# Taking the mean of the attention output out of the output weights, and the layer-norm statistics onto ScalarE

## Chip, cores and metric

The kernel runs on one core of one Trainium2 chip. The metric is device time in microseconds (us) of one execution; lower is better. TensorE is called PE, VectorE DVE, ScalarE ACT, GpSimd POOL and SyncE SP, as in the profile. SP issues nearly all the DMAs; ACT issues a few.

## What is computed

The input `x` has 2048 tokens of 1024 channels, in float32. One block of single-head attention with head size 256 is followed by a gated feed-forward layer (1024 to 2752 to 1024). Each has a layer norm (without gain or shift) before it and a second one on its output, ahead of the residual sum:

```python
def _layernorm(x, axis=-1, eps=1e-05):
    m = jnp.mean(x, axis=axis, keepdims=True)
    v = jnp.var(x, axis=axis, keepdims=True)
    return (x - m) / jnp.sqrt(v + eps)
...
    x = x + _layernorm(_L0_attn_ref(_layernorm(x, axis=-1), L0_attn_Wqkv, L0_attn_bqkv, L0_attn_Wo, L0_attn_bo), axis=-1)
    x = x + _layernorm(_L0_ffn_ref(_layernorm(x, axis=-1), L0_ffn_W_gate, L0_ffn_W_up, L0_ffn_W_down), axis=-1)
```

The attention ends with `out @ Wo + bo`, and the feed-forward layer computes `(silu(x @ W_gate.T) * (x @ W_up.T)) @ W_down.T`. In what follows, *a* is the attention output of a token (after `Wo` and `bo`), *x1* is `x + layernorm(a)`, and *xn* is `layernorm(x1)`, the input of the feed-forward layer.

## The kernel before

All large products run as three float32r matmuls on operands that are split into a high and a low part: `split` (L111, L112) copies the high part on ACT (a CAST) and subtracts it on DVE. So each weight or activation block that PE reads costs one ACT and one DVE instruction.

**Stages.** First come the projections to q, k and v with the statistics of `x` (row mean and scale of each token, kept in SBUF by `m_of` and `r_of`), up to about 140 us. Then comes attention over 16 tiles of 128 tokens (`i`, up to about 410 us). Then the feed-forward layer runs in two halves of 1024 tokens; in each, `gate_up` runs over ten pairs `p` of weight blocks (in the first half about 410 to 795 us), and `run_down` follows. Products of the feed-forward layer are arranged as in Strassen's scheme, which needs sums of blocks on DVE (L883, L791 to L794).

**One attention tile.** `scores`, `softmax` (exp on ACT, L443), `turn` (PE transposes, then split), `attend`, `turn_o` (L478, split at L480 and L481) and `proj` (the product with `wo_s`, the split `Wo`; DVE scales it and adds `bo_s`, L491) give *a*. `wo_split` makes `wo_s` from `wr`, pinned into the programs of tiles 0 and 1.

**From a to xn.** `out_stats` takes mean and scale of *a* by `norm_stats` (two bn_stats L118, bn_aggr L121, a small add L122 on DVE, a power L123 on POOL, then L499 on POOL). `residual` applies them on ACT (L505), adds `x` (L506), stores *x1* (L507), takes the statistics of *x1* in the same way, and writes *xn* on ACT (L510). `spread` (ACT's DMA, L597) and `gather` (SP's DMA, L600) pass *xn* through DRAM, `xpose` transposes it on DVE (L604, pinned) and stores it (L606).

The first eight tiles (`t < EARLY`, with EARLY = 8) do this inside the attention loop, two tiles behind. The last eight store *a* to DRAM (`at_d`) and are done later, one in each of the pairs p = 1 to 8 of the first half of the feed-forward layer. There `ahead(p)` transposes tile p-1 and loads *a* (L1308) and `x` (L1309) of tile p into two rooms that swap roles at each p, so that the load of *a* needs the room that `xpose` has just read, and the load of `x` the one that `xpose` wrote and L606 stores. `behind(p)` runs `residual` and `spread`, and `between(p)` the `gather`.

**One pair of gate_up.** Fourteen products of twelve matmuls each use four PSUM banks, `ag, au, cg, cu`. The part that matters here:

```python
        prod(ag, wg, "S3", "T3", False)
        nc.scalar.copy(g22, ag)
        add(g22, cg, g22)
        silu(g22, g22)
        prod(au, wu, "S3", "T3", False)
        nc.scalar.copy(u22, au)
        ...
        prod(ag, wg, "A22", "T4", False)
```

The copies L931 (`g22`) and L935 (`u22`) read a bank that PE needs again one product later.

**Order.** The order on each engine is fixed when the program is built, by a scheduler with its own timeline of the kernel, except where an instruction is pinned (`pin`, `tc.keep_in_program_order`). Weight loads and their splits are queued by `Feeder`, as buffers come free. The chip then runs each engine's instructions in that order.

Of the kernel before, what the change touches and what calls it, by code (L numbers as in the profile page):

```python
# [10 lines left out]
AF = mybir.ActivationFunctionType  # L11
ALU = mybir.AluOpType
# [5 lines left out]
C = 1024  # L18
# [6 lines left out]
TB = G // P  # L25
# [3 lines left out]
EPS = 1e-5  # L29
# [5 lines left out]
def block_kernel(ctx, tc, x, xt, wqk, wqk_t, wv, bqk, bv, wo, bo, wgu, wlast, wd, out):  # L35
# [12 lines left out]
    nc = tc.nc  # L48
# [4 lines left out]
    def tl(p, shape, dt, name):  # L53
        return p.tile(shape, dt, tag=name, name=name, bufs=1)
# [7 lines left out]
    bo_s = tl(cpool, [P, C], F32, "bo_s")  # L62

    mhalf = tl(cpool, [P, 16], F32, "mhalf")[:, 0:1]
# [7 lines left out]
    def small_tile():  # L72
        small_n[0] += 1
        return small[small_n[0] % NSM]

    bank_pool = pool("banks", space=PSUM)
    bank = [tl(bank_pool, [P, 512], F32, f"bank{i}") for i in range(8)]
# [29 lines left out]
    def f32(ap):  # L107
        return ap.bitcast(F32)

    def split(hi, lo, src, lo_engine=None):  # L110
        nc.scalar.copy(hi, src)  # L111
        (lo_engine or nc.vector).tensor_tensor(lo, src, f32(hi), ALU.subtract)  # L112

    def norm_stats(halves, pin=None):

        s = small_tile()
        for i, h in enumerate(halves):
            b = nc.vector.bn_stats(s[:, 6 * i : 6 * i + 6], h)  # L118
            if pin:
                pin(b)  # L120
        nc.vector.bn_aggr(s[:, 12:14], s[:, 0:12])  # L121
        nc.vector.tensor_scalar(s[:, 14:15], s[:, 13:14], EPS, None, ALU.add)  # L122
        nc.gpsimd.tensor_tensor(s[:, 15:16], s[:, 14:15], mhalf, ALU.pow)  # L123
        return s[:, 12:13], s[:, 15:16], s

    def mm3(o, w, m, first, last, pin=lambda i: i):

# [38 lines left out]
    pin = tc.keep_in_program_order  # L166
    L, R = slice(0, 512), slice(512, 1024)
# [19 lines left out]
    def m_of(g, tb):  # L187
        return yg[g][:, 2 * tb : 2 * tb + 1]
# [69 lines left out]
    def scores(i, j, pin=lambda i: i):  # L258

        cols = slice((i % TB) * P, (i % TB + 1) * P)  # L260
        q = qa if i < TB else qs[(i // TB) % 2]
        for d in range(2):
            k = kT(d, j)
            mm3(bank[j], (q[:, d, 0, cols], q[:, d, 1, cols]), (k[:, 0, :], k[:, 1, :]), d == 0, d == 1, pin)
        nc.vector.tensor_reduce(ys[i % 4][:, j : j + 1], bank[j], AX.X, ALU.max)
# [8 lines left out]
    def wv_pair(j):  # L274

        r = wv_raw[j // 2][:, (j % 2) * 512 : (j % 2) * 512 + 512].rearrange("p (c f) -> p c f", f=D)
        return wv_s[:, 2 * j : 2 * j + 2, 0, :], wv_s[:, 2 * j : 2 * j + 2, 1, :], r
# [54 lines left out]
    for c in range(2):  # L332
        h, l, r = (t[:, c, :] for t in wv_pair(0))
# [86 lines left out]
    wo_s = wvo.rearrange("p a b c -> p (a b c)").rearrange("p (d h c) -> p d h c", d=2, h=2)  # L420
    pT = [a2[:, 4 * i : 4 * i + 4, :, :].rearrange("p a b c -> p (a b c)").rearrange("p (k h q) -> p k h q", h=2, q=P) for i in range(2)]
    o_s = [f2[4][:, 0:D], f2[4][:, D:]]
    EARLY = 2 * TB
# [5 lines left out]
    def q_load(g):  # L429
        nc.sync.dma_start(qraw, q_d[g])  # L430

    def q_split(g, pin=lambda i: i):
        q = qs[g % 2]
        pin(nc.scalar.copy(q[:, :, 0, :], qraw))
        nc.vector.tensor_tensor(q[:, :, 1, :], qraw, f32(q[:, :, 0, :]), ALU.subtract)

    def softmax(i):

        s = ys[i % 4]
        nc.vector.tensor_reduce(s[:, 4:5], s[:, 0:4], AX.X, ALU.max)  # L440
        nc.vector.tensor_scalar(s[:, 5:6], s[:, 4:5], -1.0 / 16.0, None, ALU.mult)
        for j in range(4):
            nc.scalar.activation(p_s[:, j * 512 : j * 512 + 512], bank[j], AF.Exp, bias=s[:, 5:6], scale=1.0 / 16.0, accum_out=s[:, 8 + j : 9 + j])  # L443
        nc.vector.tensor_reduce(s[:, 12:13], s[:, 8:12], AX.X, ALU.add)
        nc.vector.reciprocal(s[:, 13:14], s[:, 12:13])

    def turn(i, j):

        b = bank[(4, 7)[j % 2]]
        for n in range(4):  # L450
            k = 4 * j + n
            nc.tensor.transpose(b[:, n * P : (n + 1) * P], p_s[:, k * P : (k + 1) * P], ident)  # L452
        d = pT[i % 2][:, 4 * j : 4 * j + 4, :, :]
        split(d[:, :, 0, :], d[:, :, 1, :], b.rearrange("p (n q) -> p n q", n=4))
# [29 lines left out]
    def proj(i):  # L484
# [8 lines left out]
            nc.sync.dma_start(at_d[i], a)  # L493
        return m

    def out_stats(t, a):

        m, r, s = norm_stats([a[:, 0:512], a[:, 512:1024]], tc.keep_in_program_order if t >= EARLY else None)
        nc.gpsimd.tensor_scalar(s[:, 16:17], m, r, -1.0, ALU.mult, ALU.mult)  # L499
        return r, s  # L500

    def residual(t, a, xt, st=None, pin=lambda i: i):

        r, s = st or out_stats(t, a)
        pin(nc.scalar.activation(a, a, AF.Identity, bias=s[:, 16:17], scale=r))  # L505
        (nc.gpsimd if t >= EARLY else nc.vector).tensor_tensor(xt, xt, a, ALU.add)  # L506
        nc.sync.dma_start(x1_d[t].rearrange("(g s) c -> s g c", g=4), xt)  # L507
        m, r, s = norm_stats([xt[:, 0:512], xt[:, 512:1024]])
        nc.gpsimd.tensor_scalar(s[:, 16:17], m, r, -1.0, ALU.mult, ALU.mult)
        nc.scalar.activation(a, xt, AF.Identity, bias=s[:, 16:17], scale=r)  # L510

    cols = lambda g, n: load_cols(g, 2 * n, 2, col_room[g][n])
    parts = lambda g: [x_parts(g, 2 * n, 2, col_room[g][n]) for n in range(4)]
# [59 lines left out]
    wr = [tl(wpool, [P, C], F32, f"wr{i}") for i in range(2)]  # L573
# [4 lines left out]
    xe = tl(spool, [P, C], F32, "xe")  # L578
# [8 lines left out]
    for d in range(2):  # L587
        nc.sync.dma_start(wr[d], wo[d * P : (d + 1) * P, :])

    def wo_split(d):  # L590
        pin(nc.scalar.copy(wo_s[:, d, 0, :], wr[d]))
        pin(nc.vector.tensor_tensor(wo_s[:, d, 1, :], wr[d], f32(wo_s[:, d, 0, :]), ALU.subtract))


    def spread(t, a):

        nc.scalar.dma_start(xn_d[t].rearrange("(i s) (g c) -> i s g c", i=4, g=4).rearrange("i s g c -> (s g) i c"), a.rearrange("p (i c) -> p i c", i=4))  # L597

    def gather(t, b):
        nc.sync.dma_start(b, xn_d[t])  # L600

    def xpose(t, a, b):

        pin(nc.vector.transpose(a.rearrange("p (j g s) -> p j g s", j=8, g=4), b.rearrange("p (g j c) -> p j g c", g=4, j=8)))  # L604
        d = xT_d[t // TB][:, (t % TB) * P : (t % TB + 1) * P]
        nc.sync.dma_start(d.rearrange("(j p) t -> p j t", p=P), a.rearrange("p (j t) -> p j t", j=8))  # L606
# [29 lines left out]
    L, R = slice(0, 512), slice(512, 1024)  # L636
# [22 lines left out]
    pin = tc.keep_in_program_order  # L659
# [77 lines left out]
    class Slot:  # L737
        t = None
# [466 lines left out]
    for i in range(NT):  # L1205
        more = i + 1 < NT
        if i % TB == 0 and TB <= i < NT - TB:
            q_load(i // TB + 1)
        if 3 <= i < EARLY + 3:
            gather(i - 3, pair[i % 3][1])  # L1210
        turn(i, 0)
        turn(i, 1)
        if i == NT - 1:
            for f in order[:2]:
                f.use()
            for f, r in zip(order[4:6], f4[2:4]):
                f.load(r)
        if more:
            scores(i + 1, 0)
            scores(i + 1, 1)  # L1220
        turn(i, 2)
        turn(i, 3)
        if more:
            scores(i + 1, 2)
            scores(i + 1, 3)
            softmax(i + 1)

        if i < 2:
            wo_split(i)
        if i == 1:  # L1230
            q_load(1)
        if i == 2:
            q_split(1, pin)
        if i % TB == 0 and TB <= i < NT - TB:
            q_split(i // TB + 1, pin)
        if 2 <= i < EARLY + 2:
            residual(i - 2, *pair[(i - 2) % 3], sts[i - 2], pin)
            spread(i - 2, pair[(i - 2) % 3][0])
        if i < 3:
            nc.sync.dma_start(pair[i][1], x[i * P : (i + 1) * P, :])  # L1240
        if i == NT - 1:
            for f in order[2:5]:
                f.use()
            for f, r in zip(order[6:8], (wr[1], f4[1])):
                f.load(r)
        if i > 0:
            turn_o(i - 1)
        attend(i)
        if i > 0:
            proj(i - 1)  # L1250
        if 3 <= i < EARLY + 3:
            xpose(i - 3, *pair[i % 3])
        if 3 <= i < EARLY:
            nc.sync.dma_start(pair[i % 3][1], x[i * P : (i + 1) * P, :])
        if 0 < i <= EARLY:
            sts[i - 1] = out_stats(i - 1, pair[(i - 1) % 3][0])
        cb = i - EARLY - 3
        if 0 <= cb < 4:
            first_sums(cb, *room[cb % 2])
        if 0 <= cb + 1 < 4:  # L1260
            first_load(cb + 1, *room[(cb + 1) % 2])
        if i == NT - 4:
            feed.pump()
        if i == NT - 2:
            for n in range(2):
                slots.free(flat(a2[:, 2 * n : 2 * n + 2, :, :]))
            feed.pump()
            order = [t2[0], t13[0], t13[1], t13[2], t2[1], t13[3]] + t4
            spare = f4[2], f4[3], wr[1], xe
            for f, r in zip(order, spare):  # L1270
                f.load(r)
# [129 lines left out]
```

## Time and profile before

| | |
|---|---|
| median of 3 runs | 1645.23 us (1644.34 to 1645.7) |
| the profiled execution | 1644.92 us, of which span 1643.1 us |
| PE busy | 1633.6 us (99%) |
| DVE busy | 1122.5 us (68%) |
| ACT busy | 718.2 us (44%) |
| POOL busy | 108.7 us (7%) |
| granted PE clock | 1.000 over the span |

The span runs from the first to the last instruction on the core; 1.82 us of the profiled execution's time lie around it. Busy time is the time in which an engine's own instructions ran. In a timeline each row has the start, the duration, the engine and line, and in brackets how long the engine had been idle before and what ended that idle time.

### The profile page before, as it was taken

How to read it: one execution, taken by the hardware profiler on the slowest of the kernel's cores; microseconds unless marked ns; L12 is line 12 of the kernel's file. 1: busy time of each engine (PE TensorE's matmuls, PEld its weight loads, DVE VectorE, ACT ScalarE, POOL GpSimd, SP SyncE). 2: the span in 40 equal slices, each digit the busy share in tenths (PEclk: the TensorE clock that was granted, in tenths of full speed). 3: DMA queues.
4: the chain of work that ended last, by engine and by line, in shares of the span. 5: the costliest groups of instructions: out<-in, count | busy, mean ns of one | idle time of the engine just before them, and what ended most of it. 6: DMA issues, size and time to landing. Idle time of an engine off the chain costs nothing.

```text
span 1643.1 us, 20860 instructions
## 1 busy us (share of the span) xinstructions
PE 1633.6 (99%) x7576; PEld 1361.1 (83%) x7576; DVE 1122.5 (68%) x1676; ACT 718.2 (44%) x1061; POOL 108.7 (7%) x157
## 2 busy tenths in 40 slices
PE   9999999999999999999999999999999999999998
PEld 8888888888888888888888888888888888888887
DVE  6656787778778888787577458855666655455458
ACT  5663445436444444433465344433333333354342
POOL 3120000000011111120000001100000000000001
PEclk9999999999999999999999999999999999999999
DMA  9452145556657777677477657532222333686663
GB/s 324 164 178 69 52 158 189 167 199 210 232 172 242 252 252 246 227 237 264 156 250 248 195 182 236 199 104 96 97 96 96 103 103 121 242 260 195 192 190 121
DMA packets 148184, 300.38 MB, mean 183 GB/s; under 512 B 14576, under 2 KB 39792, under 8 KB 148080
## 3 DMA queue, kind: packets, MB, share of 16 engines
q1 hardware_dynamic: 138480, 288.69, 53.1%
q10 hardware_dynamic: 9600, 10.36, 2.0%
q8 instruction: 59, 0.97, 0.2%
q14 instruction: 45, 0.37, 0.1%
HBM read 206.70 MB, written 92.29 MB: 182 GB/s over the span
## 4 chain that ended last, share of the span: by engine, by line
PE 94%; DVE 2%; DMA 2%; issue 1%; ACT 0%; POOL 0%; SPq 0%; POOLq 0%; DVEq 0%; ACTq 0%
PE bank L869 71%; PE bank L128 4%; PE bank L130 4%; PE bank L129 4%; PE bank L468 3%; PE bank L469 2%; PE bank L452 2%; PE bank L246 1%; PE bank L247 1%; PE bank L311 1%; DVE a L112 0%; DMA f<-xn_d 0%; DMA f<-wv 0%; DMA xn_d<-f 0%; PE bank L1056 0%
## 5 line engine op out<-in xcount | busy, mean ns | idle before, releaser
L869 PE MATMUL bank<-a 128*128 128x512 f32 (+1 forms) x960 | 226.4, 386 | 0.0
L869 PE MATMUL bank<-xb,a 128*128 128x512 f32 x912 | 212.5, 389 | 0.1
L869 PEld LDWEIGHTS bank<-a 128*128 128x128 f32 x960 | 179.1, 188 | 36.6
L869 PEld LDWEIGHTS bank<-xb,a 128*128 128x128 f32 x912 | 170.9, 188 | 35.8 <-DVE a L112 0.5
L111 ACT CAST a<-f2p 128x1024 fp32r<-128x1024 f32 (+2 forms) x123 | 106.9, 869 | 124.7 <-PE bank L869 89.5
L112 DVE TENSOR_TENSOR a<-f2p,a 128x1024 fp32r<-128x1024 f32 (+2 forms) x123 | 122.4, 995 | 44.1 <-ACT a L111 37.7
L869 PE MATMUL bank<-kx,a 128*128 128x512 f32 x612 | 145.2, 389 | 0.0
L869 PEld LDWEIGHTS bank<-kx,a 128*128 128x128 f32 x612 | 114.9, 188 | 23.8
L112 DVE TENSOR_TENSOR a<-f,a 128x1024 fp32r<-128x1024 f32 (+1 forms) x70 | 79.9, 1141 | 61.3 <-ACT a L111 59.0
L869 PE MATMUL bank<-wvo 128*128 128x512 f32 (+1 forms) x498 | 120.9, 387 | 0.0
L869 PEld LDWEIGHTS bank<-wvo 128*128 128x128 f32 x498 | 93.0, 188 | 18.9
L111 ACT CAST a<-f 128x1024 fp32r<-128x1024 f32 (+1 forms) x70 | 57.6, 823 | 101.1 <-PE bank L869 96.2
L869 PE MATMUL bank<-a,a 128*128 128x512 f32 x420 | 99.6, 389 | 0.3 <-ACT p_s L931 0.3
L869 PE MATMUL bank<-kx,wvo 128*128 128x512 f32 x420 | 99.3, 389 | 0.0
L883 DVE TENSOR_TENSOR xi<-bank,xi 128x512 f32<-128x512 f32 (+1 forms) x90 | 60.9, 681 | 48.5 <-PE bank L869 42.2
L869 PEld LDWEIGHTS bank<-a,a 128*128 128x128 f32 x420 | 78.8, 188 | 17.1 <-ACT p_s L931 0.8
L869 PEld LDWEIGHTS bank<-kx,wvo 128*128 128x128 f32 x420 | 78.8, 188 | 16.3
L112 DVE TENSOR_TENSOR wvo<-f,wvo 128x1024 fp32r<-128x1024 f32 (+1 forms) x47 | 54.6, 1162 | 53.1 <-ACT wvo L111 53.1
L869 PE MATMUL bank<-a1b,wvo 128*128 128x512 f32 x360 | 86.6, 389 | 0.0
L883 DVE TENSOR_TENSOR p_s<-bank,p_s 128x512 f32<-128x512 f32 x80 | 53.9, 681 | 46.7 <-PE bank L869 42.9
L869 PEld LDWEIGHTS bank<-a1b,wvo 128*128 128x128 f32 x360 | 67.6, 188 | 14.0
L869 PE MATMUL bank<-kx 128*128 128x512 f32 (+1 forms) x339 | 78.5, 387 | 0.0
(341 smaller groups left out, 3063.7 us busy)
## 6 DMA issues: line engine op xcount, KB each, us to landing
f2p<-wgu SPq DMA_DIRECT2D x41, 512.0 KB, 5.5
f<-x SPq DMA_DIRECT2D x28, 512.0 KB, 6.0
f<-wgu SPq DMA_DIRECT2D x22, 512.0 KB, 3.5
wr<-wgu SPq DMA_DIRECT2D x21, 512.0 KB, 4.9
hd_S<-xi SPq DMA_DIRECT2D x42, 256.0 KB, 4.4
f<-wd SPq DMA_DIRECT2D x20, 512.0 KB, 4.1
td_T<-f SPq DMA_DIRECT2D x40, 256.0 KB, 5.0
f2p<-td_T SPq DMA_DIRECT2D x40, 256.0 KB, 3.0
```

Source lines behind the costliest of these rows:

```text
L111: nc.scalar.copy(hi, src)
L112: (lo_engine or nc.vector).tensor_tensor(lo, src, f32(hi), ALU.subtract)
L128: pin(nc.tensor.matmul(o, w[0], m[0], start=first, stop=False))
L129: pin(nc.tensor.matmul(o, w[0], m[1], start=False, stop=False))
L130: return pin(nc.tensor.matmul(o, w[1], m[0], start=False, stop=last))
L246: pin(nc.tensor.matmul(b, xg[:, c, 0, cols], wv_s[:, c, :, :].rearrange("p a f -> p (a f)"), start=(c == 0), stop=False))
L247: pin(nc.tensor.matmul(b[:, D:], xg[:, c, 1, cols], wv_s[:, c, 0, :], start=False, stop=(c == 7)))
L452: nc.tensor.transpose(b[:, n * P : (n + 1) * P], p_s[:, k * P : (k + 1) * P], ident)
L468: nc.tensor.matmul(b, p[:, k, 0, :], vt(k).rearrange("p h d -> p (h d)"), start=(k == 0), stop=False)
L469: nc.tensor.matmul(b[:, D:], p[:, k, 1, :], vt(k, 0), start=False, stop=(k == NKB - 1))
L869: one = nc.tensor.matmul(o, w[i], m[j], start=first and n == 0, stop=last and n == 2, skip_group_check=chained)
L883: nc.vector.tensor_tensor(o, a, b, op)
```

## The change

`wo_split` takes each row's mean out of `Wo`, and `center_bo` the mean out of `bo`, so that *a* comes out of the projection with mean zero. Its norm then needs only a sum of squares, which ACT takes with Square and an accumulated sum (into a scratch `xe`, or for the late tiles in two halves into the PSUM banks 4 and 5). DVE applies the scale and adds `x` in one instruction, for the late tiles also, where POOL added before. As *x1* is `x` plus something of mean zero, its mean is that of `x` from the first stage (`m_of`); a Square with the bias -mean gives its variance. `norm_stats` is gone.

```diff
-    def norm_stats(halves, pin=None):
-        s = small_tile()
-        for i, h in enumerate(halves):
-            b = nc.vector.bn_stats(s[:, 6 * i : 6 * i + 6], h)
-            if pin:
-                pin(b)
-        nc.vector.bn_aggr(s[:, 12:14], s[:, 0:12])
-        nc.vector.tensor_scalar(s[:, 14:15], s[:, 13:14], EPS, None, ALU.add)
-        nc.gpsimd.tensor_tensor(s[:, 15:16], s[:, 14:15], mhalf, ALU.pow)
-        return s[:, 12:13], s[:, 15:16], s
...
+    def scale_of(s):
+        nc.gpsimd.tensor_scalar(s[:, 2:3], s[:, 0:1], 1.0 / C, EPS, ALU.mult, ALU.add)
+        nc.gpsimd.tensor_tensor(s[:, 3:4], s[:, 2:3], mhalf, ALU.pow)
+        return s[:, 3:4]
     def out_stats(t, a):
-        m, r, s = norm_stats([a[:, 0:512], a[:, 512:1024]], tc.keep_in_program_order if t >= EARLY else None)
-        nc.gpsimd.tensor_scalar(s[:, 16:17], m, r, -1.0, ALU.mult, ALU.mult)
-        return r, s
-    def residual(t, a, xt, st=None, pin=lambda i: i):
-        r, s = st or out_stats(t, a)
-        pin(nc.scalar.activation(a, a, AF.Identity, bias=s[:, 16:17], scale=r))
-        (nc.gpsimd if t >= EARLY else nc.vector).tensor_tensor(xt, xt, a, ALU.add)
+        s = small_tile()
+        if t < EARLY:
+            nc.scalar.activation(xe, a, AF.Square, accum_out=s[:, 0:1])
+        else:
+            for k, h in enumerate((L, R)):
+                nc.scalar.activation(bank[4 + k], a[:, h], AF.Square, accum_out=s[:, k : k + 1])
+            nc.gpsimd.tensor_tensor(s[:, 0:1], s[:, 0:1], s[:, 1:2], ALU.add)
+        return scale_of(s)
+    def residual(t, a, xt, r=None, pin=lambda i: i):
+        r = out_stats(t, a) if r is None else r
+        pin(nc.vector.scalar_tensor_tensor(xt, a, r, xt, ALU.mult, ALU.add))
         nc.sync.dma_start(x1_d[t].rearrange("(g s) c -> s g c", g=4), xt)
-        m, r, s = norm_stats([xt[:, 0:512], xt[:, 512:1024]])
-        nc.gpsimd.tensor_scalar(s[:, 16:17], m, r, -1.0, ALU.mult, ALU.mult)
-        nc.scalar.activation(a, xt, AF.Identity, bias=s[:, 16:17], scale=r)
+        s, m = small_tile(), m_of(t // TB, t % TB)
+        nc.gpsimd.tensor_scalar(s[:, 4:5], m, -1.0, None, ALU.mult)
+        nc.scalar.activation(a, xt, AF.Square, bias=s[:, 4:5], accum_out=s[:, 0:1])
+        r = scale_of(s)
+        nc.gpsimd.tensor_tensor(s[:, 5:6], s[:, 4:5], r, ALU.mult)
+        nc.scalar.activation(a, xt, AF.Identity, bias=s[:, 5:6], scale=r)
...
+    def minus_mean(t):
+        s = small_tile()
+        pin(nc.scalar.activation(t, t, AF.Identity, accum_out=s[:, 0:1]))
+        nc.gpsimd.tensor_scalar(s[:, 1:2], s[:, 0:1], -1.0 / C, None, ALU.mult)
+        return s[:, 1:2]
     def wo_split(d):
-        pin(nc.scalar.copy(wo_s[:, d, 0, :], wr[d]))
-        pin(nc.vector.tensor_tensor(wo_s[:, d, 1, :], wr[d], f32(wo_s[:, d, 0, :]), ALU.subtract))
+        m = minus_mean(wr[d])
+        pin(nc.scalar.activation(wo_s[:, d, 0, :], wr[d], AF.Identity, bias=m))
+        pin(nc.vector.scalar_tensor_tensor(wo_s[:, d, 1, :], wr[d], m, f32(wo_s[:, d, 0, :]), ALU.add, ALU.subtract))
+    def center_bo():
+        m = minus_mean(bo_s)
+        pin(nc.scalar.activation(bo_s, bo_s, AF.Identity, bias=m))
...
         if i < 2:
             wo_split(i)
+        if i == 0:
+            center_bo()
```

In the built program the scheduler also moves other instructions. PE has the same matmuls, in the same order in the feed-forward layer; within the attention tiles some groups change places.

## The prediction

> **What bounds the kernel now.** I read the page's busy times first, then what PE waited for.
>
> ```profile
> span 1643.1 us, 20860 instructions
> PE 1633.6 (99%) x7576; PEld 1361.1 (83%) x7576; DVE 1122.5 (68%) x1676; ACT 718.2 (44%) x1061; POOL 108.7 (7%) x157
> ```
> ```profile
> PE bank L272 <- POOL ident masks.py:199: 1.4, 1, 1.4
> PE bank L128 <- DVE oTs L481: 0.8, 2, 0.4
> PE bank L869 <- ACT p_s L931: 0.3, 1, 0.3
> ```
>
> PE is idle for 9.5 us: 1.4 at the start, about 7 after its last matmul, and little else. The change leaves PE's matmuls as they are, so work that it takes off DVE or POOL can give back no more than the small waits, about 1.1 us. It can cost as much as it makes PE wait. I call 0.2% (3.3 us) the least that a measurement of this kernel can tell from no change.
>
> So I looked for the places where PE has least cover. The last wait above shows one: the copy L931, whose bank PE needs one product later. In the timelines, pair p = 2 (first two fences: PE, ACT) and pair p = 9 (third: ACT, PE) read:
>
> ```profile
> 494.31 5.60 PE L869 MATMUL bank<-kx,wvo 128*128 128x512 f32 x24
> 499.75 5.60 PE L869 MATMUL bank<-a,a 128*128 128x512 f32 x24
> ```
> ```profile
> 489.07 0.59 ACT L922 COPY p_s<-bank 128x512 f32<-128x512 f32 x1 [2.13 <-PE bank L869]
> 491.56 1.06 ACT L111 CAST a<-f 128x1024 fp32r<-128x1024 f32 x1 [1.91 <-PE bank L869]
> 494.28 1.76 ACT L111 CAST a<-f2p 128x1024 fp32r<-128x1024 f32 x2 [1.66 <-PE bank L869]
> 497.23 0.59 ACT L931 COPY p_s<-bank 128x512 f32<-128x512 f32 x1 [1.19 <-PE bank L869]
> 499.95 0.59 ACT L935 COPY xi<-bank 128x512 f32<-128x512 f32 x1 [2.13 <-PE bank L869]
> ```
> ```profile
> 766.18 0.58 ACT L931 COPY p_s<-bank 128x512 f32<-128x512 f32 x1
> 766.81 1.43 PE L869 MATMUL bank<-a,a 128*128 128x512 f32 x5 [0.34 <-ACT p_s L931]
> ```
>
> A product lasts 2.72 us (L931 to L935). L931 ends at 497.82 and PE returns to its bank at 499.75: 1.9 us to spare. At p = 9 the copy came late, ended at 766.76, and PE began 0.05 later. Two rows of DVE, two of SP and the landing of the load of *a* complete what I need:
>
> ```profile
> 488.80 1.25 DVE L604 STREAM_TRANSPOSE f<-f 128x1024 f32<-128x1024 f32 x1 [3.62 <-DMA f<-xn_d]
> 492.72 1.22 DVE L112 TENSOR_TENSOR a<-f,a 128x1024 fp32r<-128x1024 f32 x1
> ```
> ```profile
> 490.07 0.37 SPq L606 DMA_DIRECT2D xT_d<-f  x1
> 490.54 0.53 SPq L1308 DMA_DIRECT2D f<-at_d  x1
> ```
> ```profile
> L1308 SPq DMA_DIRECT2D f<-at_d x8: 326/532/539, 425.8 to 720.9; - x8
> DMA to landing us min/median/max: 4.3/5.4/6.8
> ```
>
> **Wo and bo.** Two CASTs of 1.05 become three summing Identities (1.05 and 0.19 for reading the sum, as L205) and three biased ones (1.25, as L510), with three POOL instructions of 0.2: 5.4 us more ACT. The first `Wo` half was split by 160.1 and PE first uses it at 170.3; the new chain adds about 2.5. The second was ready at 172.5 and used from 175.9; in the built order PE takes some other products before it, and the chain ends near 174.8. Cost nothing; without that cover, up to 1 us once.
>
> **The eight early tiles.** DVE loses four bn_stats of 0.68, two aggregates of 0.20 and two adds of 0.14, 3.4 us a tile; the add of `x` (1.22) stays as one scalar_tensor_tensor of like size. ACT loses an Identity of 1.25 and gains two Squares of 1.24 and 1.34 with their reads: 1.3 more. ACT's Identity for *xn* now waits behind its own Square and three POOL instructions, about 1.4 us (0.19 and 0.57 as L209 and L210, 0.27 as L509, and hops); before it waited for DVE and POOL, 26.5 us over 15 times. Behind it in ACT's queue stand the copy of `attend`'s result and the casts of the turned probabilities. Of PE's two waits for L481, the first (0.36 at 183.5) stays, since the built order leaves PE 0.1 us less work ahead of it; the second (0.44 at 231.8) goes, since more stands ahead of `proj` there. Together -0.4 us; the bounds are -0.8 and, if the new ACT wait reaches PE in some tiles, +3.
>
> **The eight late tiles, off PE.** DVE loses the 3.4 and gains the 1.22; POOL loses eight adds of 2.40, and with them goes what they did to DVE (a 512-wide L112 took 2.49 beside one, 0.69 alone). All of that lies beside PE's products and gives nothing.
>
> **The late tiles, on PE's path.** Here the built order decides. In pairs 2 to 8 ACT now runs: L922, the two half Squares of *a*, both L111 casts of 1024, the Square of *x1*, a 512 cast, L931, the Identity for *xn*, L935. DVE runs L604, the sums, L112, L791, the new scalar_tensor_tensor, L792. ACT takes them in this order, so L931 now stands behind the landing of *a*. I follow it at p = 2, where DVE was free for L604 at 488.80 - 3.62 = 485.18:
> - L604 ends 1.25 later, and L1308 is issued 0.49 after that (490.54 - 490.05), then lands after 5.4 and wakes ACT in 0.1: 7.24.
> - Two Squares at 0.67 each (the spacing of L443's 512-wide sums): 1.34. They wait at ACT's head from 489.7 on, and behind them the casts.
> - The cast to DVE's L112: 1.16 (491.56 to 492.72). L112 to L791: 1.25 (492.72 to 493.97). L791: 0.72.
> - The scalar_tensor_tensor and the hop to ACT: 1.32. Its `x` (L1309, about 5.3 after L604's start, landing 5.0 to 6.8) comes at about the same time, and POOL's chain before it.
> - Square of *x1* 1.20 (L207, less overlap), cast 0.52, L931 0.59.
>
> That is 7.24 + 8.10 = 15.34 after 485.18, while PE comes at 499.75, 14.57 after it, less the 0.05: a wait of 0.82 us. DVE's start and PE's return repeat at 38.08 each pair, so the wait does, in seven pairs: 5.7. L604 isn't held by the gather there, since `spread` now leaves at about 502.5, and 7.5 and 4.1 later the gather has landed, 8 us before L604. Only at p = 2 is it late: tile 8's `spread` leaves about 2 us earlier than before (477.4), so L604 starts near 486.8: 1.6 more (bounds 0 and 3.6).
>
> Landing is what I know least, since the load moves 2 to 5.5 us ahead into other traffic. The rows bound it: 4.3 (the first load, with little around it) gives no wait at all; the seven others have 5.3, 5.4, 5.4, 6.3, 5.5, 5.3 and 6.8, by which the sum is 7.9. I take the median, since the same store and stores of sums still surround it. The Trainium skill's "DMA: Bandwidth & Descriptors", section "Anatomy of one DMA", fits a DMA (on another issue path) as 2.0 us plus its bytes over 436 GB/s: an estimate of 3.2 us for 512 KB, by which L931 would be in time and the total that of the first rival below; the trace's 4.3 to 6.8 speak against it.
>
> L935 then follows the Identity, which waits for the Square's read and POOL. Undisturbed it ends in time (about 2.2 after L931; PE needs it 2.7 after). A small POOL power took 1.46 beside a DVE subtraction of 1.22 (474.2); if that falls in, 0.5 more a pair. I take 0.1, so 0.7 (0 to 3.5).
>
> SP's queue: the gather L600 moves ahead of two hidden stores and two weight loads, and SP waits in it to about 510. The stores were issued at 502.7 and 506.4 and their buffers are rewritten from 517; the loads came at 511.8 anyway. Nothing. At p = 9 no late tile is left and L604 isn't held: the 0.5 us by which PE fell behind its pace there goes.
>
> **Sum.** 1644.92 (span 1643.1 and 1.82 around it) + 5.7 + 1.6 + 0.7 - 0.5 - 0.4 = 1652.0. The profiled execution is 0.3 below the median of the runs, so I predict 1652.3.
>
> **Rivals.** *All hidden.* The load of *a* lands within 4.6 us of issue, and L931 stays in time. Only the small waits change: 1643.8 to 1645.5, not slower. For it: L1308's 4.3 once, and 1.9 us of room before; it decides from 4.6 downwards. Against it: seven of eight landings. *Attention loses instead.* In tiles 3 to 5 the turned probabilities now have 3.2 to 3.4 us of PE work ahead of their use (4.6 or more before) and need 1.9 with free engines (cast 0.59, subtraction 0.69, hops); an Identity held 1.4 with its own 1.2 behind it can make that 3.3 to 4.5, so up to 1.5 a tile, 1 to 5 in all: 1646 to 1650. It decides once that Identity is held while a turned block waits. Against it: DVE, the busier engine there, has 3.4 us less a tile. *A gain* of over 3.3 us has only 1.1 us of waits to come from.
>
> **How the numbers follow.** Forecast 0.70, all hidden 0.22, attention alone 0.06, a gain 0.02. The forecast's own range is 1647 (landing 5.0, no p = 2 excess) to 1660 (landings as in the rows 7.9, 3.6 at p = 2, 3.5 for L935, on 1644.9). The range goes to 1645.0, into the first rival, leaving out about half of it, and to 1660. Slower by over 0.2%: 0.76; within 0.2%: 0.22; faster: 0.02.
>
> **What would show it.** PE waits for ACT at L931's successor in seven pairs, 0.5 to 2 us each, most at p = 2; the half Squares show idle time ended by the DMA of *a*; L604's idle time (3.6 to 6.8) is gone after p = 2; PE's wait of 0.34 near 767 is gone. If the Squares start without waiting for the load, or the waits sum to under 3 us, the step from landing to L931 is wrong; if PE waits in attention, the second rival is right.

## The result, and the profile after

The changed kernel takes 1650.32 us (median of 6 runs, 1649.76 to 1651.12), the kernel before 1644.85 us beside it (1644.33 to 1645.73). The ratio is 1.0033, with a 95% interval from 1.0020 to 1.0046: slower by some 5.5 us, in the forecast direction, and 2.0 us under the predicted time. The profiled execution took 1651.02 us. The head of the page:

```profile
span 1649.2 us, 20820 instructions
PE 1637.3 (99%) x7576; PEld 1360.0 (82%) x7576; DVE 1079.4 (65%) x1556; ACT 739.9 (45%) x1132; POOL 88.9 (5%) x192
```

DVE lost 43 us of work and POOL 20, ACT gained 22, and the span is 6.1 us longer. PE has the same 7576 matmuls, yet is "busy" for 3.7 us more. What PE waited for (total, times, longest):

```profile
PE bank L260 <- POOL ident masks.py:199: 1.4, 1, 1.4
PE bank L880 <- ACT xi L942: 1.3, 2, 1.1
PE bank L880 <- ACT p_s L942: 0.8, 2, 0.5
PE bank L880 <- DVE a L112: 0.6, 1, 0.6
PE bank L116 <- DVE oTs L469: 0.5, 1, 0.5
```

Lines have moved: L942 is the copy of `g22` (L931 before), L946 that of `u22` (L935), L880 the matmul (L869), L615 the transpose (L604), L1321 the load of *a* (L1308). Only 2.1 us stand against L942 here and nothing against L946. The rest hides in the busy time, since the ends of matmuls are modelled. The list of what the weight loads (PEld) waited for names both copies, 8.8 us in all, since their idle time begins earlier (0.73 in pair 2, where PE shows 0.31). In the kernel before, its only entry for either copy was L931, with 0.8:

```profile
PEld bank L880 <- ACT xi L942: 3.7, 5, 1.6
PEld bank L880 <- ACT p_s L942: 2.1, 3, 0.9
PEld bank L880 <- ACT xi L946: 1.7, 4, 0.5
PEld bank L880 <- ACT p_s L946: 1.3, 3, 0.5
```

I count a pair from the first matmul of its product with `kx` and `a` (488.33 in pair 2 here, 488.87 before), called "the product with `kx`" below. PE in pair 2, with the weight load that L946 holds, and the same product in pair 5:

```profile
493.77 5.60 PE L880 MATMUL bank<-kx,wvo 128*128 128x512 f32 x24
499.68 6.09 PE L880 MATMUL bank<-a,a 128*128 128x512 f32 x24 [0.31 <-ACT p_s L942]
502.71 2.63 PEld L880 LDWEIGHTS bank<-a,a 128*128 128x128 f32 x12 [0.44 <-ACT xi L946]
505.60 0.62 PE L880 MATMUL bank<-a1b,wvo 128*128 128x512 f32 x2
...
617.14 6.07 PE L880 MATMUL bank<-a,a 128*128 128x512 f32 x24 [1.14 <-ACT xi L942]
```

Twenty-four matmuls are two products and last 5.44 us from start to start, in every pair of the kernel before. Here the first start comes 499.68 - 493.77 - 5.44 = 0.47 late, and the group itself lasts 505.60 - 499.68 = 5.92, 0.48 too long: a second wait in its middle, where PE needs the bank that L946 copies. I measure both waits from starts in what follows, as "the wait at g22" and "the wait at u22". In pairs 2 to 8 of the kernel after:

| | p=2 | 3 | 4 | 5 | 6 | 7 | 8 | sum |
|---|---|---|---|---|---|---|---|---|
| at g22 (L942) | 0.47 | 0.28 | 0.20 | 1.31 | 0.35 | 0.61 | 0.18 | 3.40 |
| at u22 (L946) | 0.48 | 0.47 | 0.49 | 0.47 | 0.47 | 0.45 | 0.46 | 3.29 |

Pair 2 starts 0.54 earlier than before. So PE is 3.40 + 3.29 - 0.54 = 6.15 late at the start of pair 9 (761.57 against 755.43). The 0.50 that the kernel before lost in pair 9 goes, with 0.13 that followed it, and 0.6 is lost at the start of the second half (the wait for L112 above): 6.1 in all.

ACT in pair 2, with the chain that ends at the two copies:

```profile
491.66 0.60 ACT L497 ACTIVATE bank<-f 128x512 f32<-128x512 f32 x1 [2.55 <-DMA f<-at_d]
...
492.91 1.03 ACT L111 CAST a<-f 128x1024 fp32r<-128x1024 f32 x1
...
497.39 1.15 ACT L508 ACTIVATE f<-f,small 128x1024 f32<-128x1024 f32 x1 [2.49 <-DVE f L504]
...
498.54 0.61 ACT L111 CAST a<-f2p 128x512 fp32r<-128x512 f32 x1
499.05 0.58 ACT L942 COPY p_s<-bank 128x512 f32<-128x512 f32 x1
500.94 1.25 ACT L511 ACTIVATE f<-f,small 128x1024 f32<-128x1024 f32 x1 [1.32 <-POOL small L510]
502.09 0.56 ACT L946 COPY xi<-bank 128x512 f32<-128x512 f32 x1
```

The half Square of *a* (L497) waits at ACT's head for the load of *a*; the Square of *x1* (L508) waits for DVE; L942 stands behind both and ends at 499.63, while PE would have come at 499.21. Then the Identity (L511) waits for POOL, with L946 behind it. DVE's transpose, which starts the chain, and its wait for `x` in pair 5; then the load of *a* (durations of the issue, then of the landing):

```profile
484.56 1.24 DVE L615 STREAM_TRANSPOSE f<-f 128x1024 f32<-128x1024 f32 x1
...
498.41 1.22 DVE L112 TENSOR_TENSOR a<-f2p,a 128x1024 fp32r<-128x1024 f32 x1
...
613.47 1.28 DVE L504 SCALAR_TENSOR_TENSOR f<-f,small,f 128x1024 f32<-128x1024 f32 x1 [0.85 <-DMA f<-x]
```
```profile
L1321 SPq DMA_DIRECT2D f<-at_d x8: 326/572/573, 425.4 to 720.8; - x8
DMA to landing us min/median/max: 4.0/5.4/5.5
```

The transpose no longer waits for the gather, even in pair 2. In pair 5 the load of `x` was the later one: it is issued only after the store of the transposed tile has landed, took 7.4 us itself, and made that pair's wait 1.31. Last, POOL in pair 2, the small operations of the first norm and of the second:

```profile
493.37 0.19 POOL L486 TENSOR_SCALAR small<-small 128x1 f32<-128x1 f32 x1
493.64 0.56 POOL L487 TENSOR_TENSOR small<-small,mhalf 128x1 f32<-128x1 f32 x1
498.72 0.96 POOL L486 TENSOR_SCALAR small<-small 128x1 f32<-128x1 f32 x1 [4.52 <-ACT f L508]
499.76 0.88 POOL L487 TENSOR_TENSOR small<-small,mhalf 128x1 f32<-128x1 f32 x1
```

The same two operations take 0.75 us where DVE is idle as they begin, and 1.84 beside its L112 and L805; in pairs 3 to 8 they read the same within 0.02. That is the wait at u22.

### The profile page after: what moved, and what is told of

The parts are those of the page before. It is cut to its first block, busy times and chain, and to the rows that moved or that the text cites. A ratio compares the mean times of both kernels' runs of the same rounds, so it can differ in the third digit from the quotient of the medians.

```text
span 1649.2 us, 20820 instructions
## 1 busy us (share of the span) xinstructions
PE 1637.3 (99%) x7576; PEld 1360.0 (82%) x7576; DVE 1079.4 (65%) x1556; ACT 739.9 (45%) x1132; POOL 88.9 (5%) x192
## 4 chain that ended last, share of the span: by engine, by line
PE 92%; DMA 3%; DVE 3%; issue 1%; ACT 1%; POOL 0%; POOLq 0%; DVEq 0%; SPq 0%; ACTq 0%
PE bank L880 68%; PE bank L116 4%; PE bank L118 4%; PE bank L117 4%; PE bank L456 3%; PE bank L457 2%; PE bank L440 2%; PE bank L234 1%; DMA f<-x 1%; PE bank L299 1%; PE bank L235 1%; DMA xT_d<-f 1%; PE bank L1067 0%; PE bank L1066 0%; PE bank L452 0%
## 5 line engine op out<-in xcount | busy, mean ns | idle before, releaser
L880 PE MATMUL bank<-a 128*128 128x512 f32 (+1 forms) x960 | 226.4, 386 | 0.0
L880 PE MATMUL bank<-xb,a 128*128 128x512 f32 x912 | 212.5, 389 | 0.6 <-DVE a L112 0.6
L880 PEld LDWEIGHTS bank<-a 128*128 128x128 f32 x960 | 179.1, 188 | 36.5
L880 PEld LDWEIGHTS bank<-xb,a 128*128 128x128 f32 x912 | 170.9, 188 | 36.4 <-DVE a L112 1.1
L112 DVE TENSOR_TENSOR a<-f2p,a 128x1024 fp32r<-128x1024 f32 (+2 forms) x123 | 122.3, 994 | 42.0 <-ACT a L111 35.4
L880 PE MATMUL bank<-kx,a 128*128 128x512 f32 x612 | 145.2, 389 | 0.0
L880 PEld LDWEIGHTS bank<-kx,a 128*128 128x128 f32 x612 | 114.9, 188 | 23.8
L112 DVE TENSOR_TENSOR a<-f,a 128x1024 fp32r<-128x1024 f32 (+1 forms) x70 | 65.7, 938 | 102.2 <-ACT a L111 94.7
L880 PE MATMUL bank<-wvo 128*128 128x512 f32 (+1 forms) x498 | 120.9, 386 | 0.0
L880 PEld LDWEIGHTS bank<-wvo 128*128 128x128 f32 x498 | 93.0, 188 | 18.9
L880 PE MATMUL bank<-a,a 128*128 128x512 f32 x420 | 102.9, 394 | 2.5 <-ACT xi L942 1.3
L880 PE MATMUL bank<-kx,wvo 128*128 128x512 f32 x420 | 99.2, 389 | 0.0
L880 PEld LDWEIGHTS bank<-a,a 128*128 128x128 f32 x420 | 77.7, 188 | 24.6 <-ACT xi L942 3.7
L880 PEld LDWEIGHTS bank<-kx,wvo 128*128 128x128 f32 x420 | 78.8, 188 | 16.4
L112 DVE TENSOR_TENSOR wvo<-f,wvo 128x1024 fp32r<-128x1024 f32 (+1 forms) x47 | 54.8, 1165 | 54.9 <-ACT wvo L111 54.9
L880 PE MATMUL bank<-a1b,wvo 128*128 128x512 f32 x360 | 86.8, 389 | 0.0
L880 PEld LDWEIGHTS bank<-a1b,wvo 128*128 128x128 f32 x360 | 67.6, 188 | 14.0
L880 PE MATMUL bank<-kx 128*128 128x512 f32 (+1 forms) x339 | 78.5, 387 | 0.0
```

The source lines that it names most:

```text
L880: one = nc.tensor.matmul(o, w[i], m[j], start=first and n == 0, stop=last and n == 2, skip_group_check=chained)
```

## Experiments

Theory: PE loses its time behind the two ACT copies of the late pairs, because new work of the late tile stands ahead of them in ACT's order. Rivals: the attention tiles (or the centring of `Wo`) lose it; or DVE or the loads do, whatever stands in ACT's queue. Each group of runs shared one chip and the runs of the kernel before on it, which differ: 1648.52 us in the first group (32 runs, 1645.68 to 1651.06), 1644.79 in the second, 1644.74 in the third. So kernels are compared within a group. The two sums are those of the profiled execution, over pairs 2 to 9. For two kernels that execution is far from the median: "Identity alone" was profiled at 1650.63, 1.7 above it, and "one small POOL operation" at 1647.17, 1.8 below.

| | median us | against before (95%) | at g22 | at u22 |
|---|---|---|---|---|
| **first group** | | | | |
| new norms in early tiles only | 1647.84 | 0.9998 (0.9990 to 1.0007) | 2.56 | 0.74 |
| new norms in late tiles only | 1652.08 | 1.0022 (1.0012 to 1.0031) | 3.46 | 3.32 |
| Square and Identity behind both copies | 1645.25 | 0.9982 (0.9973 to 0.9990) | 0.45 | 0.57 |
| Identity alone behind both copies | 1648.89 | 1.0006 (0.9997 to 1.0014) | 3.93 | 0.99 |
| **second group** | | | | |
| the changed kernel again | 1650.79 | 1.0037 (1.0024 to 1.0049) | 3.45 | 3.26 |
| own rooms | 1643.73 | 0.9992 (0.9984 to 1.0001) | 0 | 0 |
| one small POOL operation | 1648.98 | 1.0023 (1.0014 to 1.0032) | 2.93 | 0.97 |
| late tiles only, Square behind | 1645.49 | 1.0003 (0.9994 to 1.0012) | 0.55 | 0.32 |
| **third group** | | | | |
| before, with own rooms | 1644.82 | 0.9999 (0.9990 to 1.0008) | 0 | 0 |
| own rooms, no centring | 1644.44 | 0.9996 (0.9987 to 1.0005) | 0 | 0 |
| own rooms again | 1643.83 | 0.9992 (0.9983 to 1.0000) | 0 | 0 |

**One half of the change at a time.**

```diff
...
+    def out_stats(t, a):
+        return (out_stats_new if t < EARLY else out_stats_old)(t, a)
+
+    def residual(t, a, xt, st=None, pin=lambda i: i):
+        (residual_new if t < EARLY else residual_old)(t, a, xt, st, pin)
```

> The new statistics are used for the eight early tiles only; the late tiles keep the old norms (bn_stats, an Identity for the scaled a, the add on GpSimd). The centring of Wo and bo stays. Theory (PE loses its time behind two ACT copies of the late pairs, of g22 and of u22): none of those waits, only the attention tiles' gain of about 0.5 us, so 1644.4 us (1643.8 to 1645.2), like before. Rival (attention or the chain that centres Wo loses the time): about 1650, as the whole change has. Second rival (both halves of the change cost): between, 1646 to 1648.

Measured 1647.84, above the expected time, and as long as the kernel before on this chip. The number lies in the second rival's range, but that range was set against a kernel before of 1644.9, not of 1648.5. There were waits at g22, but not the changed kernel's: here the late tiles are the old ones. Pair 6:

```profile
641.46 0.32 SPq L645 DMA_DIRECT2D f<-xn_d  x1
...
645.42 1.25 DVE L649 STREAM_TRANSPOSE f<-f 128x1024 f32<-128x1024 f32 x1 [8.14 <-DMA f<-xn_d]
...
652.56 0.58 ACT L976 COPY xi<-bank 128x512 f32<-128x512 f32 x1
...
653.19 3.02 PE L914 MATMUL bank<-a,a 128*128 128x512 f32 x12 [1.19 <-ACT xi L976]
```

The gather was issued 0.5 us after the pair's product with `kx` began; in the kernel before it was 3.0 us ahead of it (638.15 against 641.19). All behind it slides, to the copy of `g22` (L976). This run is inconclusive in its time, and it showed me something that I had missed (see the last section).

The reverse, in the same two functions:

```diff
+        return (out_stats_old if t < EARLY else out_stats_new)(t, a)
...
+        (residual_old if t < EARLY else residual_new)(t, a, xt, st, pin)
```

> The reverse: the early tiles keep the old norms, the late tiles have the new ones. The centring of Wo and bo stays. Theory: PE waits behind the copies of g22 and u22 in pairs 2 to 8 as in the whole change, about 3.4 + 3.3 us less 0.5 at p = 9, so 1650.3 to 1651.5 us. Rival (attention loses): 1644.9, like before.

1652.08, 0.6 above the expected range, with both sums as in the changed kernel (3.46 and 3.32 against 3.40 and 3.29). By these sums the late tiles alone bring the loss, and the rival that attention loses it falls; the times could say so only beside the changed kernel, which was not run on this chip.

**The order on ACT.**

```diff
-            residual(late(p), a, b)
-            spread(late(p), a)
+            held[p] = residual(late(p), a, b)
+
+    def tail(p):
+        a, b = rooms(p)
+        with tc.issue_after(held['u22']):
+            held[p]()
+        spread(late(p), a)
```

Now `residual` goes only up to the store of *x1* and returns the rest (the Square, the small operations and the Identity), which `tail` calls.

> The whole change, but in the late tiles the Square of x1, the three GpSimd instructions behind it and the Identity for xn are issued on ACT after the copy of u22. Nothing is left out. The half Squares of a and the casts stay ahead of the copy of g22. Theory (it is the queue order on ACT, with a chain that is only some tenths to 1.3 us too long, that costs): the Square's 1.15 no longer stands ahead of the g22 copy and the Identity's chain no longer ahead of the u22 copy, so both waits go, at most 0.2 us of it stays in pair 5 where x landed late: 1644.3 us (1643.8 to 1645.3). Rival (the wait is for DVE or for the loads, whatever ACT has in its queue): DVE and the loads are as they were, so most of the 5.5 us stays, 1649 to 1651.

1645.25 (runs from 1644.83 to 1646.73), at the upper end of the expected range, and the sums fall from 3.46 and 3.32 (late tiles only, same chip) to 0.45 and 0.57. Its pair 2:

```profile
498.99 0.58 ACT L948 COPY p_s<-bank 128x512 f32<-128x512 f32 x1
499.69 0.59 ACT L952 COPY xi<-bank 128x512 f32<-128x512 f32 x1
500.17 1.16 ACT L510 ACTIVATE f<-f,small 128x1024 f32<-128x1024 f32 x1
...
501.50 0.19 POOL L486 TENSOR_SCALAR small<-small 128x1 f32<-128x1 f32 x1 [6.98 <-ACT f L510]
501.77 0.55 POOL L487 TENSOR_TENSOR small<-small,mhalf 128x1 f32<-128x1 f32 x1
...
504.34 1.24 ACT L513 ACTIVATE f<-f,small 128x1024 f32<-128x1024 f32 x1
```

DVE and the loads were as late as before (the first half Square waited until 491.99, 3.38 after the product with `kx`, and 3.33 in the changed kernel); the order behind them differs. The rival that the order doesn't matter falls.

> The whole change, but in the late tiles the Identity for xn alone is issued after the copy of u22; the Square of x1 stays ahead of the copy of g22. Nothing is left out. Theory (two separate terms, some 3.4 us at the copy of g22 and some 3.3 at that of u22, the second from GpSimd's small operations and the Identity): the second goes and the first stays, 1647.0 us (1646.4 to 1647.8), and PE's first product of the two keeps its step of 0.2 to 1.3 a pair, the second loses its 0.47. Rival (the second wait is only the echo of the first, both from one late chain): either both stay (1650) or, with a shorter tail, little goes (1649 and more).

(The edit is the same with the Square left in its place.) 1648.89, 1.1 above the range (why stays open), 3.6 above the run with both moved and 3.2 below the late tiles alone: the first term stays (3.93), the second falls to 0.99. So there are two terms, one for the Square and one for the Identity. What is left at u22 is 0.13 to 0.18 a pair, and about as much follows a wait at g22 in every run, so it belongs to the first.

**The changed kernel again, and rooms of their own.**

> The changed kernel itself, unaltered, beside the altered ones. The run with the late tiles alone took 1652.1 us and its sums of waits were 3.5 us (copy of g22) and 3.3 us (copy of u22). Theory: the same waits here, and about 0.5 us less in the attention tiles: 1650.3 to 1652.0 us. Rival (the early tiles' part costs as well): above 1652.5.

1650.79, in the range.

```diff
-        return f4[2 + p % 2], f4[3 - p % 2]
+        return (f4[3], f4[2]) if p % 2 else (wr[1], bo_s)
...
-        if late(p - 1):
-            a, b = rooms(p - 1)
-            xpose(late(p - 1), a, b)
         if late(p):
             a, b = rooms(p)
             nc.sync.dma_start(a, at_d[late(p)])
             nc.sync.dma_start(b, x[late(p) * P : (late(p) + 1) * P, :])
+        if late(p - 1):
+            a, b = rooms(p - 1)
+            xpose(late(p - 1), a, b)
```

> The whole change, with rooms of their own for the late tiles: they alternate between two pairs of buffers, and the loads of a and x are issued ahead of the transpose of the tile before, so that neither waits for that transpose or for its store. In the built order ACT then takes the copies of g22 and u22 ahead of the Square of x1. Nothing is left out. Theory (the chain from the loads to the two copies is only some tenths to 1.3 us too long): both waits go, 1644.8 us (1644.0 to 1645.6), with about 3 us and more between each copy and the product that needs its bank. Rival (earlier loads collide with the gather and the weight loads, and PE then waits for weights or for the transpose instead): 1646.5 or more, with PE's waits at other lines.

1643.73, 7.1 us below the changed kernel and 0.3 below the expected range. The waits:

```profile
PE bank L260 <- POOL ident masks.py:199: 1.4, 1, 1.4
PE bank L116 <- DVE oTs L469: 0.5, 1, 0.5
PE bank L880 <- DVE a L112: 0.4, 1, 0.4
PE bank L299 <- DVE wvo L322: 0.2, 1, 0.2
```

No wait is left in the late pairs, but not for the reason that I gave. A pair's loads still follow a transpose, since each pair of rooms takes every second tile: in pair 2 the load of *a* was issued at 489.04, later than in the changed kernel (486.25). With the rooms every tile runs one pair sooner (two stores of *x1* lie ahead of pair 2, where the changed kernel has one), and the built order has casts and copies ahead of the Square. That the first brought about the second is my reading of the order, not tested. ACT in pair 2:

```profile
493.51 1.05 ACT L111 CAST a<-f2p 128x1024 fp32r<-128x1024 f32 x1 [1.67 <-PE bank L880]
495.97 0.60 ACT L497 ACTIVATE bank<-f 128x512 f32<-128x512 f32 x1 [1.40 <-DMA f<-at_d]
...
497.72 0.57 ACT L942 COPY p_s<-bank 128x512 f32<-128x512 f32 x1
499.13 0.59 ACT L946 COPY xi<-bank 128x512 f32<-128x512 f32 x1 [0.84 <-PE bank L880]
500.42 1.15 ACT L508 ACTIVATE f<-f,small 128x1024 f32<-128x1024 f32 x1 [0.70 <-DVE f L504]
```

L942 ends at 498.29, which is 10.2 after the pair's product with `kx` began (488.06), and in the changed kernel 11.3 (499.63 and 488.33), though the load came later. That fits the order on ACT as the cause; this run alone doesn't separate it from the tiles' earlier place. This is the best version that I found; against the kernel before it is 0.9992, which is at the edge of what the runs can tell.

**POOL's small operations.**

```diff
-        r = scale_of(s)
+        r = s[:, 0:1] if t >= EARLY else scale_of(s)
         nc.gpsimd.tensor_tensor(s[:, 5:6], s[:, 4:5], r, ALU.mult)
```

> The whole change, but in the late tiles the second norm has one small GpSimd operation in place of three: the mean's scale and the power are left out, so xn of these eight tiles isn't normed. ACT's and DVE's order in the pairs is as in the whole change. Theory (the copy of u22 is late because two small GpSimd operations beside DVE take 0.96 and 0.88 and hold the Identity ahead of it): the Identity starts about 1.8 us earlier, and the wait at the copy of u22 falls from 3.3 to 0.7 us or less in sum; that at the copy of g22 stays at 3 to 4.5: 1648.0 us (1647.2 to 1649.3). Rival (the Identity's own 1.25 ahead of the copy is enough): 2.5 us or more of the second sum stays: 1650 to 1651.5.

1648.98, in the range. The sum at u22 falls from 3.26 to 0.97, or 0.13 to 0.15 a pair, which is what follows a wait at g22. ACT's order is the changed kernel's:

```profile
498.94 0.97 POOL L510 TENSOR_TENSOR small<-small 128x1 f32<-128x1 f32 x1 [4.85 <-ACT f L508]
...
499.95 1.24 ACT L511 ACTIVATE f<-f,small 128x1024 f32<-128x1024 f32 x1
501.10 0.57 ACT L946 COPY xi<-bank 128x512 f32<-128x512 f32 x1
```

So the Identity's own length ahead of the copy costs next to nothing here, and its wait for POOL does cost. The one small operation that is left takes 0.97, like the first one there, as DVE's L112 runs from 498.65 to 499.87.

**What the early tiles and the centring are worth.**

> The early tiles keep the old norms; the late tiles have the new ones with the Square of x1, its small operations and the Identity issued after the copy of u22 (as in the run that took 1645.25 us with the new norms in all tiles). The centring of Wo and bo stays. The difference of the two is what the early tiles' part of the change is worth, without the waits of the late pairs. Theory (attention gains 0.4 to 0.5 us): 1645.7 us (1645.3 to 1646.2). Rival (attention loses 1 us or more by its new waits): 1644.3 or less.

1645.49, in the range. Against the run of the late tiles alone it differs only by what `tail` puts behind the copies, and the sums fall from 3.46 and 3.32 to 0.55 and 0.32, though on another chip. The like run with new norms in all tiles was on another chip, so the times decide little. In the traces, the first product with `kx` of pair 1 starts at 450.22 and 450.61 with the old norms in the early tiles and `Wo` centred, and at 449.70 to 451.44, with a median of 450.2, in the eight with the new ones. A gain of 0.4 can't be told from that spread; a loss of 1 us or more isn't there.

> The change with own rooms (1643.73 us, no waits in the late pairs), without the part that takes the mean out of Wo and bo: that work is left out, so the mean of the projection stays in the norms. Theory (the chain for Wo lies beside other products of PE and costs nothing): the same as with the centring, 1643.7 us (1643.3 to 1644.2). Rival (the chain delays the first products with Wo by up to 1 us or more, or holds ACT ahead of the first turned blocks): 1642.9 or less.

1644.44, 0.2 above the range and 0.6 above the kernel with the centring on the same chip: leaving it out gains nothing. Why it was longer was not followed up. Its trace has a wait of 0.8 us in attention that the other lacks, the other has one of 0.5 there that this one lacks, and the two profiled executions are only 0.1 apart.

**The kernel before, with own rooms.**

> The kernel before with the late tiles' own rooms alone: two pairs of buffers in turn, and the loads of a and x issued ahead of the transpose of the tile before; norms, Wo and bo as before. In the traces of the old late tiles one tile hands on to the next in a loop of about 38.0 us (load of a at 2.1 after the pair's first matmul of its product with kx, store of x1 at 19.4, spread at 26.8, gather at 34.3, transpose at 38.4, next load at 40.2), as long as PE's 38.08 a pair, and the gather drifts from -4.1 to -1.9 us against PE in seven pairs, or to +0.5 where DMAs are slower. Theory (that loop makes PE wait for the old kernel's copy of g22, by 0.5 us in one run and by some us in another): with the loop cut, the gather keeps its place against PE, there is no wait at that copy at p = 9 either, and the runs spread by under 1.5 us: 1644.2 us (1643.7 to 1644.8). Rival (the drift comes from elsewhere, the old norms are just longer): like before, with its spread.

1644.82, at the upper end of the range and no different from before on this chip. In the trace the wait in pair 9 is gone and the gather, at -5.7 to -3.8 against the product with `kx` in pairs 2 to 8, has no trend, but a wait of 1.1 for a split at the start of the second half makes up for it. Ten of its 11 runs lie within 1.5 us, as the theory had it, and one at 1647.63, which it had not. What the drift costs could not be shown in time, since the kernel before took 1644.74 here and so lost little to it.

> The change with own rooms once more, as the measure for the two others on this chip: 1643.7 us (1643.2 to 1644.6) whatever this chip's run of the kernel before gives, since no PE wait is left in the late pairs for slower DMAs to lengthen. Rival (its gain against the kernel before is that of the chip): it moves with the kernel before.

1643.83, as on the other chip; but the kernel before was the same on both, so this does not test the rival.

## Why the prediction was right, and by which steps

**L931 behind the landing of *a*: right, 0.35 a pair too high.** The transpose-to-copy chain in pair 2 was to last 15.34 us and lasted 499.63 - 484.56 = 15.07: landing and wake 7.10 (7.24), Squares 1.25 (1.34), cast to L112 1.06 (1.16), the Square of *x1* 1.15 (1.20), the rest within 0.07 each. PE came 14.65 after the transpose's start (14.57). That makes 0.47 for the 0.82 predicted, and over seven pairs 3.40 for 5.7. The sign that I had named was 0.5 to 2 a pair, most in pair 2: five of the seven are under 0.5 and the most is in pair 5, so the sum passed its least value of 3 by only 0.4. But for the first load (4.0), all landed in 5.3 to 5.5, so the median was the right choice and the estimate of 3.2 that I set against it was not. What I called "at about the same time", the load of `x`, became the later one in pair 5 and gave the largest wait.

**The 1.6 of pair 2: wrong.** Tile 8's `spread` left at 438.62, not 2 us but 38.8 earlier than before (477.38), so its *xn* was gathered long in time and L615 started with no idle time. This and the 2.3 of the step above are the 3.9 that the first term was too high.

**L935 behind the Identity: mis-sized, 3.29 for 0.7.** The step named the mechanism, a small POOL operation lengthened beside DVE, with 0.5 a pair and a bound of 3.5, and then took 0.1. The rows for "undisturbed" (L209 and L210, 0.19 and 0.57) were ones without a DVE operation beside them; in the pairs DVE ran a two-input operation each time. The kernel before had rows for that in its own late pairs: the power L123 took 0.92 and 1.46 in each of the pairs 2 to 8. That the term is worth 2.3 on its own, with 1.0 following from g22, the run with one small operation shows. The two errors, -3.9 and +2.6, partly cancel by luck, so the total is better than its terms.

A rule bears on it. In these rows POOL's operation beside L112, which reads two SBUF operands, ended 0.05 after it (499.68 and 499.63), and the same operation took 0.19 beside a DVE addition that reads a PSUM bank (501.50 in the run with the Square moved; the addition ran from 501.29 to 501.98). The Trainium skill, "SBUF — State Buffer", section "SBUF: two separate sides", says that a DVE operation with two SBUF inputs and a GpSimd operation that reads SBUF exclude each other for the whole of the one that starts first. Where DVE starts first the trace agrees, and by that rule the row beside a busy DVE was the one to take. Where POOL starts first it doesn't show it: in pair 2 L112 began at 493.97, inside POOL's L487 (493.64 to 494.20), and took its usual 1.23.

**The rest.** The late tiles' relief of DVE and POOL gave nothing, as said. Pair 9's wait went (0.50 of 0.50). Attention and `Wo` gave 0.54 in this one execution (-0.4 and nothing), within the spread of 1.7 that other executions show. *All hidden* needed a landing under 4.6, and those of the seven pairs were 5.3 or more. *Attention loses* is refuted by the trace of the changed kernel, which starts pair 1 0.54 earlier than before, and by the run of the late tiles alone, which has both sums.

## What to carry to other kernels

On an engine that runs in order, a new instruction costs by what stands behind it: list the copies that free PE's banks, with the time from the end of each to PE's return, and work out when everything put ahead of them can start. Price a small POOL operation beside busy DVE by the row beside busy DVE. And look at distances between starts on PE and at the waits of its weight loads: 4.6 of the 6.7 us of waits here did not stand in the list of what PE's matmuls waited for.

## What the runs showed that I had not expected

The old late tiles form a loop. Against the product with `kx` in the kernel before, the load of *a* goes at 1.7 to 3.5, the store of *x1* at 19.2 to 21.6, `spread` 7.4 later, and the gather 6.0 to 8.2 after that; the next transpose waits for the gather, and the next load for the transpose. One round takes about as long as PE's 38.08, so little pulls it back: the gather's place goes -4.08, -3.83, -3.79, -3.72, -3.04, -2.28, -1.89 in pairs 2 to 8. In pair 9, where PE waits, it goes at -3.06 again but takes 6.1 to land, where the others took 3.7 to 4.2, and one more cast stands ahead of L931. So that wait is not the drift's alone; the single late event that I had read in it is part of it. With the early norms alone, on the chip where the kernel before took 1648.52 us, the gather came between -2.97 and +0.50, and PE's two sums of waits were 3.3 us. The change breaks this loop: the store of *x1* comes at 8.7 to 9.8 and `spread` at 13.6 to 14.7, 13 us sooner, and the transpose is at -3.8 in nearly every pair. That gain bought nothing by itself here, since in the built order the tile's work then stands ahead of the two copies. What I saw of the loop on the first chip comes from the run with the early norms alone; that it made the kernel before slow there isn't shown.
